# Two metaformer layers on one core: the first transfer, products of ones at the start, and the layout of a convolution's input

## The chip, the core and the metric

The kernel runs on one core of one Trainium2 chip. The core has a matrix engine (PE), a vector engine (DVE), an activation engine (ACT), a general engine (POOL) and a queue that issues transfers (SP). The metric is the device time of one execution in microseconds, as the median of several runs.

## The reference

The input x is 8 images of 384 channels and 32 by 32 points, in float32. There are two layers, each with a token mixer and a feed-forward part:

```
# layer 0
x = x + mamba(ln_c(x))                # input product, causal 3-tap convolution, SiLU,
                                      # selective scan over 1024 tokens (16 states), gate, output product
t = tokens(x);  t = t + ffn0(ln_t(t)) # two products with binarized weights, results clipped by groups of images
# layer 1
x = x + displaced_conv(ln_c(x))       # 48 offsets, each group of 8 channels shifted, then a 5x5 Gaussian
t = tokens(x);  t = t + ffn1(ln_t(t))
```

The feed-forward parts divide the batch into five groups of one image; the images beyond the fifth get zero there. So images 0 to 4 pass through scan, ffn 0, convolution and ffn 1, and images 5 to 7 through scan and convolution alone. The displaced convolution of a channel is separable: one 32 by 32 matrix for the rows and one for the columns, which differ by group of channels.

## The kernel before

All work is first recorded as operations (`op`, `dma`) with an engine, an estimated duration, a key, and the buffers that they read and write. `Flow.run` then plays them against a model of the engines: at each moment an idle engine takes, among the operations whose inputs are ready and whose buffers are free, the one with the lowest key, and the last recorded one where keys are equal. The list `out` that results is issued as it stands, so each engine's order is fixed when the kernel is built. SP's transfers go round eight lanes, and a transfer waits for the one that took its lane before.

Work is tiled in units of one image and 512 tokens (16 units). For each unit: `load_x` brings x (768 KB) into `xn`; `layernorm` (L464 and L484 on PE for sums, L477 and L512 on ACT, L498 and L537 on DVE, L521 and L529 on ACT); `in_proj` (L645) for twelve tiles of output channels; the small convolution and SiLU (ACT L661 to L689, DVE L676); `x_proj` (L760), `prep` (L814, L824, L837); and then, for six tiles and four state groups, `scan` (POOL L868, ACT L878, DVE L893, POOL L914, DVE L927, PE L935). The feed-forward parts of finished images (L1386 and L1465 on PE, L1408 on DVE) and their convolutions are interleaved with the scan of later units; the output product is L997.

At the very start, all transfers of key -60 (x, the small vectors `cw`, `cb`, `bdt`, `dsk`, four pieces of `aneg`, and `wx`, `wdt`) are ready at once; since equal keys take the last recorded, x comes after seven of them. L617 on ACT takes the exponential of `aneg` and needs all four of its pieces.

The displaced convolution (`conv`) works on one image. DVE's L1569 transposes blocks of 32 by 32 from the layer-normed tile `tn` into three tiles `xt`, one for each 128 channels; their free dimension is ordered (row y, channel c). For each of the three, PE's L1601 multiplies with the row matrices: four products of 256 columns, each for 8 of the 32 channels of a block, so the moving operand is read as 8 channels by 32 rows, with y innermost at a step of 32 elements. L1615 (DVE) transposes the result out of PSUM, L1629 (PE) multiplies with the column matrices, L1642 (DVE) transposes back, and L1652 (POOL) adds the residual. Six convolutions lie among the scan, in five stretches, of which the last holds two images (near 865, 1490, 2165, 2785 and 3370 to 3420 us), and two more come at the end, from 3655 us. PSUM has three banks (`mm`) for all products but the scan's.

Of the kernel before, what the change touches and what calls it, by code (L numbers as in the profile page):

```python
# [146 lines left out]
OVER = {"PE": 0.0, "DVE": 0.085, "ACT": 0.1, "POOL": 0.05, "SP": 0.0}  # L147
TIE = 0
RUSH = -40.0
FILL, MARGIN, FIRST = 1e9, 0.8, 45.0  # L150
IDLE, COLD = 2.5, 5.0


class Flow:
# [4 lines left out]
    HOLD = {"exp": 0.0, "silu": 8.77, "gelu": 2.31, "softplus": 0.0}  # L159

    def __init__(self, nc):
        self.nc, self.ops, self.key, self.filler = nc, [], 0.0, None
        self.on = {
            "PE": nc.tensor,
            "DVE": nc.vector,
            "ACT": nc.scalar,
            "POOL": nc.gpsimd,
            "SP": nc.sync,
        }
# [75 lines left out]
    def run(self):  # L245
        nc = self.nc
        waiting = {e: [] for e in self.on}
        busy = {e: 0.0 for e in self.on}
        table, now, out = None, 0.0, []
        events = [0.0]  # L250
        done = []
        dma_free, landed = 0.0, [0.0] * LANES
        idle, cold = 0.0, COLD
        ends = {}
        left = len(self.ops)

        def enter(o):

            new = {}
            for b in o.bufs:  # L260
                if b.slot is None and b.ring.ordered:
                    k = new[b.ring] = new.get(b.ring, 0) + 1
                    if b.n > b.ring.given + k - 1:
                        b.ring.turn.setdefault(b.n - k + 1, []).append(o)
                        return
            insort(waiting[o.eng], (o.key, o.n, o))

        for o in self.ops:
            if o.wait == 0:
                o.ready = 0.0  # L270
                enter(o)
        while left:
            while done and done[0][0] <= now + 1e-9:
                _, _, o = heapq.heappop(done)
                for p in o.next:
                    p.wait -= 1
                    if p.wait == 0:
                        p.ready = now
                        enter(p)
                for b in o.bufs:  # L280
                    b.left -= 1
                    if b.left == 0:
                        b.ring.free.append(b.slot)
                        b.end = now
            moved = False
            nexts = []
            for e, q in waiting.items():
                if busy[e] > now + 1e-9:
                    continue
                best = None  # L290
                for i, (k, n, o) in enumerate(q):
                    if best is not None and (k > best[0] or TIE and k == best[0]):
                        break
                    if o.table is not None and o.table != table:
                        t = o.ready + (self.HOLD[o.table] if o.key > RUSH else 0.0)
                        if now < t - 1e-9:
                            nexts.append(t)
                            continue
                        k += PEN
                        if best is not None and k >= best[0]:  # L300
                            continue
                    if e == "SP" and landed[-LANES] > now + 1e-9:
                        nexts.append(landed[-LANES])
                        break
                    if Ring.open(o.bufs):
                        best = (k, i)
                if best is None:
                    continue
                o = q.pop(best[1])[2]
                for b in o.bufs:  # L310
                    if b.slot is None:
                        b.slot = b.ring.free.pop(0)
                        b.ring.given += 1
                        for p in b.ring.turn.pop(b.ring.given, ()):
                            enter(p)
                us = o.us
                if o.table is not None and o.table != table:
                    us += self.SWITCH
                    table = o.table
                if e == "PE":  # L320
                    if now - idle >= IDLE and (now > FIRST or FILL > 1e6):
                        cold = now + COLD
                    if now < cold - 1e-9:
                        us *= 2
                    if o.us > 0.5:
                        idle = now + us
                busy[e] = now + us
                if e == "SP":
                    dma_free = max(dma_free, now) + (o.lag - 1.8)
                    end = max(dma_free, now + us) + 1.8  # L330
                    landed.append(end)
                else:
                    end = now + us + o.lag
                heapq.heappush(done, (end, o.n, o))
                o.at = now
                if e == "PE":
                    ends[o.n] = now + us
                    for b in o.bufs:
                        b.at = min(b.at, now)
                out.append(o)  # L340
                left -= 1
                moved = True
            if moved:
                continue
            t = [x for x in busy.values() if x > now + 1e-9] + nexts
            if done:
                t.append(done[0][0])
            t = [x for x in t if x > now + 1e-9]
            assert t, "the instructions that are left wait for one another"
            now = min(t)  # L350
        self.end = now
        fills = self.gaps(out, ends) if self.filler else {}
        table = None
        for o in out:
            for b in fills.get(o.n, ()):
                self.filler[2](nc.tensor, b)
            if o.table is not None and o.table != table:
                table = o.table
                nc.scalar.preload_act_table_set(SETS[table])  # L359
            o.fn(self.on[o.eng])  # L360


def metaformer_flow(ctx, tc, x, mw, f0, offset, f1, out):
    nc = tc.nc
    w_in, conv_w, conv_b, w_x, w_dt, b_dt, a_log, d_skip, w_out = mw
    fl = Flow(nc)
# [202 lines left out]

    fl.key = -60  # L570
    load_x(0)
    dma(lambda: cw.ap, lambda: conv_w.rearrange("(j p) t -> p j t", p=P), (), [cw], 10)

    def small(dst, src):
# [971 lines left out]
    def conv(src, dst, dst_ap):  # L1546

        xt = [hb_r.new(2) for _ in range(KC)]
        for s in range(NS):
            last = src is x1[B - 1] and s == NS - 1  # L1550
            if last:
                tn = st[len(units) - 1]["x1"]
            else:
                tn = tn_r.new()
                dma(
                    lambda tn=tn: tn.ap,
                    lambda s=s: halves(src.ap, s),
                    [src[s * KC + k] for k in range(KC)],
                    [tn],
                    768,  # L1560
                )
            layernorm(tn, 1e-6)
            ys = slice(s * T // 32, (s + 1) * T // 32)
            for c in range(KC):

                op(
                    "DVE",
                    0.7,
                    lambda e, c=c, tn=tn, ys=ys: e.transpose(  # L1569
                        xt[c].ap.rearrange("p (y c) -> p y c", c=32)[:, ys, :],  # L1570
                        tn.ap[:, c, :].rearrange("p (y x) -> p y x", x=32),
                    ),
                    [tn],
                    [xt[c][s]],
                )
        for c in range(KC):
# [18 lines left out]
            for h in range(2):  # L1595
                acc = mm.new()

                def ups(e, lt=lts[0], acc=acc, h=h, c=c):
                    for k in (0, 1):
                        cs = slice(h * 16 + k * 8, h * 16 + k * 8 + 8)  # L1600
                        e.matmul(  # L1601
                            acc.ap.rearrange("p (c y) -> p c y", y=32)[:, k * 8 : k * 8 + 8, :],
                            lt.ap[:, 2 * h + k, :],
                            xt[c].ap.rearrange("p (y c) -> p c y", c=32)[:, cs, :],
                            start=True,
                            stop=True,
                        )

                op("PE", 1.0, ups, [lts[0], xt[c]], [acc], hold=[tr])
                hs = slice(h * T, (h + 1) * T)  # L1610

                op(
                    "DVE",
                    0.7,
                    lambda e, tr=tr, acc=acc, hs=hs: e.transpose(  # L1615
                        tr.ap[:, hs].rearrange("p (c x) -> p c x", x=32),
                        acc.ap.rearrange("p (c y) -> p c y", y=32),
                    ),
                    [acc],
                    [tr[h]],  # L1620
                )
# [139 lines left out]
```

## Time and profile before

| | |
|---|---|
| median of 3 runs | 3700.87 us (3692.59 to 3712.57) |
| the profiled execution | 3705.44 us |
| its span, first to last instruction | 3703.7 us |
| mean granted clock of PE | 0.923 |
| L1569, 45 from `tn` and 3 from `xn` | 28.5 and 2.1 us, 677 and 698 ns each |
| L1601, first and last start | 865.5 and 3692.0 us |
| POOL's L868 waiting for PE's L935 | 169.6 us |
| transfers | 777.44 MB, 74.4% of 16 engines' span |

The profile gives for each engine its busy time and share of the span. A group is all instructions of one line, engine and shape: busy us, mean ns of one, idle time ahead of them and what ended it. The chain of work that ended last is followed back from the last instruction, at each step to what released it. A matmul in float32 leaves two records. "To landing" is the time from the issue of a transfer to its data being there. All times are from the start of the span.

### The profile page before, as it was taken

Reading aid. Unit: us, or ns where it says so; the run is one execution under the profiler, and the core shown is the slowest. Engines: PE = TensorE matmul, PEld = TensorE weight load, DVE = VectorE, ACT = ScalarE, POOL = GpSimd, SP = SyncE. Lnnn points to the kernel's source line nnn. Section 1 sums busy time; section 2 is a strip of 40 time slices with the busy share of each in tenths; the row PEclk is TensorE's granted clock in tenths of the full one; section 3 lists DMA queues with packets and bytes.
Section 4 is the critical chain, followed back from the end, with each engine's and each line's share of the span. In section 5 each row is a group of like instructions: output and inputs, shape, how many; then the busy total and the mean of one; then the engine's idle time right before and its main releaser. Section 6 shows DMA issues by size and latency. Waiting matters only on the chain.

```text
span 3703.7 us, 35888 instructions
## 1 busy us (share of the span) xinstructions
PE 3189.1 (86%) x9572; PEld 1143.7 (31%) x9572; DVE 3086.6 (83%) x3080; ACT 2494.7 (67%) x3661; POOL 3157.0 (85%) x1680
## 2 busy tenths in 40 slices
PE   4777878987999897899979789998877999878988
PEld 1222223322333231333323233332223333323334
DVE  2798888878778889997987899889898888788986
ACT  4767886757667676677768757767665676765562
POOL 3879999897697998888899887989998788997893
PEclk7888979998999897999989899999988999988999
DMA  5858778696686886668587776969776787976964
GB/s 145 184 154 223 198 199 221 184 256 181 207 245 175 231 224 181 200 199 243 177 248 205 196 221 193 244 198 255 228 216 195 209 246 225 257 217 207 270 185 155
DMA packets 680820, 777.44 MB, mean 210 GB/s; under 512 B 113689, under 2 KB 434089, under 8 KB 680617
## 3 DMA queue, kind: packets, MB, share of 16 engines
q1 hardware_dynamic: 680616, 775.14, 74.4%
q8 instruction: 77, 1.26, 0.1%
q14 instruction: 127, 1.03, 0.1%
HBM read 578.45 MB, written 196.48 MB: 209 GB/s over the span
## 4 chain that ended last, share of the span: by engine, by line
PE 39%; DVE 16%; DMA 15%; POOL 12%; ACT 10%; issue 6%; SPq 2%; POOLq 0%; DVEq 0%; ACTq 0%
PE mm L1386 10%; PE mm L1465 9%; POOL t L868 8%; PE mm L645 6%; DVE dp L893 5%; PE y L935 4%; DMA dus<-via 3%; PE mm L997 3%; DVE t L893 3%; POOL t L914 3%; DVE t L927 3%; DMA dts<-via 2%; ACT L359 2%; ACT dp L878 2%; PE mm L1601 2%
## 5 line engine op out<-in xcount | busy, mean ns | idle before, releaser
L868 POOL TENSOR_TENSOR t<-dus,bc 128x1024 f32<-128x1024 f32 x768 | 1797.8, 2361 | 209.9 <-PE y L935 169.6
L914 POOL TENSOR_TENSOR t<-t,bc 128x1024 f32<-128x1024 f32 x384 | 906.8, 2362 | 99.6 <-DVE t L893 89.6
L935 PE MATMUL y<-t,sel 128*32 128x512 f32 x3072 | 554.9, 652 | 184.4 <-DVE t L927 117.8
L1465 PE MATMUL mm<-hb,w 128*128 128x512 f32 x1440 | 675.4, 609 | 28.4 <-DMA w<-w2d 12.1
L1386 PE MATMUL mm<-tn,w 128*128 128x512 f32 x1440 | 670.9, 611 | 24.7 <-DMA w<-w1d 7.5
L878 ACT ACTIVATE da<-dts,aneg 128x512 f32<-128x512 f32 x768 | 520.6, 684 | 240.7 <-DVE t L893 216.0
L878 ACT ACTIVATE dp<-dts,aneg 128x512 f32<-128x512 f32 x768 | 528.3, 688 | 207.2 <-DVE t L927 190.3
L893 DVE TENSOR_TENSOR_SCAN dp<-dp,h,t 128x512 f32<-128x512 f32 x384 | 491.3, 1279 | 71.7 <-ACT dp L878 53.5
L893 DVE TENSOR_TENSOR_SCAN dp<-dp,t 128x512 f32<-128x512 f32 x384 | 468.4, 1220 | 90.6 <-ACT dp L878 59.8
L893 DVE TENSOR_TENSOR_SCAN t<-da,h,t 128x512 f32<-128x512 f32 x384 | 481.2, 1267 | 64.2 <-POOL t L868 59.6
L893 DVE TENSOR_TENSOR_SCAN t<-da,t 128x512 f32<-128x512 f32 x384 | 458.2, 1206 | 79.5 <-POOL t L868 68.5
L359 ACT ACT_TABLE_LOAD x391 | 501.7, 1283 | 6.5
L645 PE MATMUL mm<-xn,win 128*128 128x512 f32 x900 | 439.3, 631 | 39.6 <-DMA win<-in_L_conv_in_proj_w 20.5
L927 DVE TENSOR_TENSOR t<-dp,bc 128x1024 f32<-128x1024 f32 x384 | 465.4, 1212 | 8.8 <-ACT h L920 4.0
L1465 PEld LDWEIGHTS mm<-hb,w 128*128 128x128 f32 x1440 | 264.9, 192 | 431.8 <-issue 352.7
L1386 PEld LDWEIGHTS mm<-tn,w 128*128 128x128 f32 x1440 | 269.4, 193 | 413.8 <-issue 311.5
L997 PE MATMUL mm<-z,wo 128*128 128x512 f32 x552 | 276.6, 634 | 12.2 <-DMA wo<-in_L_conv_out_proj_w 7.6
L645 PEld LDWEIGHTS mm<-xn,win 128*128 128x128 f32 x900 | 173.6, 200 | 294.7 <-issue 209.7
L1398 ACT ACTIVATE he<-mm,b 128x512 f32<-128x512 f32 x240 | 162.9, 680 | 148.9 <-PE mm L1386 141.6
L935 PEld LDWEIGHTS y<-t,sel 128*32 128x32 f32 x3072 | 83.4, 112 | 560.0 <-DVE t L927 201.1
L920 ACT COPY h<-dp 128x2 f32<-128x2 f32 x192 | 30.5, 159 | 218.4 <-DVE t L927 112.6
L1408 DVE TENSOR_REDUCE sm<-he 128x1 f32<-128x1024 f32 x120 | 144.3, 1203 | 30.8 <-ACT he L1398 30.2
(133 smaller groups left out, 3170.5 us busy)
## 6 DMA issues: line engine op xcount, KB each, us to landing
dts<-via SPq DMA_DIRECT2D x768, 128.0 KB, 4.4
dus<-via SPq DMA_DIRECT2D x768, 128.0 KB, 4.5
hd<-he SPq DMA_DIRECT2D x120, 512.0 KB, 4.7
hb<-hd SPq DMA_DIRECT2D x120, 512.0 KB, 5.9
via<-soft SPq DMA_DIRECT2D x192, 256.0 KB, 4.3
w<-w2d SPq DMA_DIRECT2D x120, 384.0 KB, 4.7
w<-w1d SPq DMA_DIRECT2D x240, 192.0 KB, 3.9
bc<-bcd SPq DMA_DIRECT2D x256, 128.0 KB, 4.7
```

Of the source, the lines that this page charges most:

```text
L359: nc.scalar.preload_act_table_set(SETS[table])
L645: e.matmul(acc.ap, w.ap[:, k, :], xn.ap[:, k, :], start=(k == 0), stop=(k == KC - 1))
L868: lambda e, t=t, du=du: e.tensor_mul(t.ap, du.ap, wide(0)),
L878: lambda e, c=c, r=r, dt=dt: e.activation(decay(c), dt.ap[:, r, :], AF.Exp, scale=aneg.ap[:, j * Q + c, g : g + 1],),
L893: e.tensor_tensor_scan(t.ap[:, r, :] if p == 0 else decay(c), decay(c), t.ap[:, r, :], 0.0 if s == 0 else hst[j][p].ap[:, g, r : r + 1], A ...
L914: op("POOL", 2.35, lambda e, t=t: e.tensor_mul(t.ap, t.ap, wide(1)), [bc], [t])
L927: lambda e, t=t: e.tensor_mul(t.ap, da[2].ap, wide(1)),
L935: e.matmul(y.ap[c * D : (c + 1) * D, :], sel.ap, ts[c // 2].ap[:, c % 2, :], start=(g == 0), stop=(g == NG - 1), tile_position=(0, c * D),)
L997: e.matmul(o.ap, flat()[:, j, :], zs[j].ap, start=(j == 0), stop=(j == JC - 1))
L1386: e.matmul(acc.ap, w.ap[:, k, :], tn.ap[:, k, :], start=(k == 0), stop=(k == KC - 1),)
L1398: lambda e, he=he, r=r, m=m, acc=acc: e.activation(he.ap[:, r, :], acc.ap, AF.Identity, bias=b1.ap[:, m : m + 1]),
L1465: e.matmul(acc.ap, w.ap[:, part * 2 + r, :], hs[m // 2].ap[:, r * T : (r + 1) * T], start=(m == 0), stop=(m == MC - 1),)
```

## The change

There are three parts.

The transfer of x for the first unit is marked (`lead`) and moved to the head of the issued list. Everything else on SP keeps its order, so the seven small transfers that stood before x now follow it directly.

`FILL` goes from 1e9 to 1.0. With that, `gaps` looks for holes of at least 1 us on PE in the model's first 45 us and puts products of ones (`keep`, 256 columns, into a free bank of `mm`, read by nobody) there. It yields four places: eight products before the first L464, eight between the first L484 and the second L464, seven between the second L484 and the first L645, and three between the third and the fourth product of L645 (26 in all). The first waits for `ones` to be set on POOL. The condition on `cold` in the model says the same as before for both values, so the modelled order stays.

In `conv`, the tile `xt` that L1601 reads is ordered (k, y, c) with four k and eight c in place of (y, c). L1569 writes it so, in runs of 8 elements; L1601's moving operand is then 256 contiguous elements; its result in PSUM is ordered (k, y, c), and L1615 reads it with y innermost at a step of 8 elements. What L1615 writes, and L1629, L1642 and L1652, are as before.

The order of the instructions on ACT and POOL is unchanged; on DVE only the shape of L1569 and L1615 differs, and on PE only the 26 products are new.

```diff
-FILL, MARGIN, FIRST = 1e9, 0.8, 45.0
+FILL, MARGIN, FIRST = 1.0, 0.8, 45.0
...
-        self.nc, self.ops, self.key, self.filler = nc, [], 0.0, None
+        self.nc, self.ops, self.key, self.filler, self.lead = nc, [], 0.0, None, None
...
-                    if now - idle >= IDLE and (now > FIRST or FILL > 1e6):
+                    if now - idle >= IDLE:
                         cold = now + COLD
...
         fills = self.gaps(out, ends) if self.filler else {}
         table = None
+        out.sort(key=lambda o: o is not self.lead)
         for o in out:
             for b in fills.get(o.n, ()):
                 self.filler[2](nc.tensor, b)
...
     fl.key = -60
     load_x(0)
+    fl.lead = fl.ops[-1]
...
                     lambda e, c=c, tn=tn, ys=ys: e.transpose(
-                        xt[c].ap.rearrange("p (y c) -> p y c", c=32)[:, ys, :],
-                        tn.ap[:, c, :].rearrange("p (y x) -> p y x", x=32),
+                        xt[c].ap.rearrange("p (k y c) -> p y k c", k=4, c=8)[:, ys],
+                        tn.ap[:, c, :].rearrange("p (y a b) -> p y a b", a=4, b=8),
                     ),
...
                     for k in (0, 1):
-                        cs = slice(h * 16 + k * 8, h * 16 + k * 8 + 8)
                         e.matmul(
-                            acc.ap.rearrange("p (c y) -> p c y", y=32)[:, k * 8 : k * 8 + 8, :],
+                            acc.ap[:, k * 256 : k * 256 + 256],
                             lt.ap[:, 2 * h + k, :],
-                            xt[c].ap.rearrange("p (y c) -> p c y", c=32)[:, cs, :],
+                            xt[c].ap[:, (2 * h + k) * 256 : (2 * h + k + 1) * 256],
...
-                        tr.ap[:, hs].rearrange("p (c x) -> p c x", x=32),
-                        acc.ap.rearrange("p (c y) -> p c y", y=32),
+                        tr.ap[:, hs].rearrange("p (k c x) -> p k c x", k=2, x=32),
+                        acc.ap.rearrange("p (k y c) -> p k c y", k=2, c=8),
```

## The prediction

> **What bounds the kernel now.** I read the busy shares first, then the chain of work that ended last, then the groups with their shapes kept apart, then the first 50 us of the timeline, and last the windows around the five places where the convolution runs.
>
> ```profile
> PE 3189.1 (86%) x9572; PEld 1143.7 (31%) x9572; DVE 3086.6 (83%) x3080; ACT 2494.7 (67%) x3661; POOL 3157.0 (85%) x1680
> PE 39%; DVE 16%; DMA 15%; POOL 12%; ACT 10%; issue 6%; SPq 2%; POOLq 0%; DVEq 0%; ACTq 0%
> PE mm L1386 10%; PE mm L1465 9%; POOL t L868 8%; PE mm L645 6%; DVE dp L893 5%; PE y L935 4%; DMA dus<-via 3%; PE mm L997 3%; DVE t L893 3%; POOL t L914 3%; DVE t L927 3%; DMA dts<-via 2%; ACT L359 2%; ACT dp L878 2%; PE mm L1601 2%
> ```
>
> No engine is the bound: PE, POOL and DVE lie within 3% of one another, and the chain changes between them. L1601, the product that the change rewrites, holds 2% of the chain (74 us by the rounded share), though all its records together are only 89.2 us busy: nearly all of it ended last somewhere.
>
> ```profile
> L1386 PE MATMUL mm<-tn,w 128*128 128x512 f32 x1440 | 670.9, 611 | 24.7 <-DMA w<-w1d 7.5 <-DVE tn L537 6.4 <-ACT he L1398 4.4
> L1601 PE MATMUL mm<-hb,lt 128*128 128x256 f32 x192 | 89.2, 615 | 13.0 <-DVE hb L1569 8.4 <-DVE hb L1642 4.1 <-DVE xn L498 0.5
> L1629 PE MATMUL mm<-hb,lt 128*128 128x128 f32 x384 | 52.9, 289 | 7.3 <-DVE hb L1615 3.2 <-ACT dp L878 1.3 <-DVE hb L1642 0.9
> L1615 DVE STREAM_TRANSPOSE hb<-mm 128x512 f32<-128x512 f32 x48 | 33.8, 706 | 24.2 <-PE mm L1601 21.7 <-ACT mm L529 2.4
> L1642 DVE STREAM_TRANSPOSE hb<-mm 128x512 f32<-128x512 f32 x48 | 32.8, 692 | 6.3 <-PE mm L1629 6.1 <-ACT da L878 0.2
> ```
>
> The column after the bar is busy us and the mean ns of one record (an fp32 product leaves two). L1601 streams 256 columns and takes 615 ns, as L1386 does for 512; L1629, which reads runs of 16, takes 289 for 128. In the timeline L1601's weight loads stand 0.43 us apart, as with 512 columns elsewhere, and L1629's 0.11. So L1601's read, one element every 128 bytes, runs at half rate.
>
> ```profile
> 5.20 0.55 SPq L217 DMA_DIRECT2D xn<-in_x  x1
> 10.87 1.93 PE L464 MATMUL mm<-xn,ones 128*32 128x512 f32 x6 [10.87 <-DMA xn<-in_x]
> 14.78 0.54 SPq L576 DMA_DIRECT2D aneg<-in_L_conv_A_log  x1
> 20.17 0.28 ACT L617 ACTIVATE aneg<-aneg 128x96 f32<-128x96 f32 x1
> 26.88 4.75 PE L645 MATMUL mm<-xn,win 128*128 128x512 f32 x6 [3.21 <-DVE xn L537]
> 31.47 2.74 PE L645 MATMUL mm<-xn,w 128*128 128x512 f32 x6
> ```
>
> At the start everything waits for x, which is the eighth transfer. The first input product takes 4.75 us at 26.88 and the next one 2.74: 4.2 us of work pass before PE's records go from 0.855 to 0.43 us apart.
>
> ```profile
> core 0: us, PE busy (x) PEld busy (x) DVE busy (x) ACT busy (x) POOL busy (x), PEclk, DMA share, GB/s
> 880.00:900.00 20.00, 19.61 (x69) 8.80 (x68) 19.17 (x24) 12.64 (x26) 13.35 (x7) 1.00 0.53 173
> 1490.00:1510.00 20.00, 19.68 (x66) 9.49 (x67) 20.00 (x25) 8.60 (x14) 19.79 (x12) 0.91 0.65 208
> 3672.00:3698.00 26.00, 20.34 (x81) 13.65 (x80) 13.40 (x21) 1.38 (x2) 9.35 (x4) 0.87 0.67 221
> ```
>
> Where a convolution lies among the scan, DVE or POOL is as full as PE; in the tail only PE is.
>
> **The product, priced.** A record goes from 0.435 us to twice L1629's spacing for twice its columns, 0.22: 0.215 saved, times 192 is 41 us of PE, 5.2 for each of eight convolutions. The group's mean should fall from 615 to about 400 ns. How much moves the end is read stage by stage.
>
> Tail (two convolutions, from 3655). I followed the timeline: L1601's eight records at 3657.61, 3665.95, 3683.34 and 3688.93 and four at 3677.25 hold DVE's L1615 or PE's own queue. The first saves 1.7; the second's gain is lost, since DVE's L1569 waits for POOL's L1652 there, which only shifts; the four at 3677.25 save 0.9, the last two groups 1.7 each. The weights (lt) of the last group are issued when the group before ends, and take 1.9 us, so they move with it. Sum 6 us.
>
> Among the scan (six convolutions). PE's gain cannot shorten a stretch below its fullest other engine. I took twelve windows of 20 us over the five stretches, and in each 20 less the larger of DVE and POOL: 1.3, 0.8, 0.2 (from 860); 0.0, 0.6 (1490); 2.1, 0.0 (2160); 2.9, 0.6 (2780); 3.5, 1.3, 1.2 (3365). That is 14.5 of PE's 31; the rest PE spends waiting for DVE or POOL. Not every idle piece of DVE waits for L1601, so I take 9, with 0 and 28 as ends (28: the chain's L1601 pieces there, some 56 us, halved).
>
> **The transposes.** L1569 now writes runs of 8, L1615 reads PSUM at 32-byte steps; 48 of each, order kept. L1642 already reads PSUM at 64-byte steps, at 692 ns against 706 for L1615's contiguous read: no price, so I take 0. [...] L1569's write has no such row; its bounds are 0 and a doubling (32 us of DVE).
>
> **x first, and the fill.** Issued at 0.74 with 5.0 to 5.5 us to landing (rows of xn), x is there by 6. But PE now begins with eight products of ones, 16 records of 256 columns, as soon as ones is set (3.2): 0.43 each cold, 0.22 warm. With the trace's 4.2 us to warm: ten cold to 7.4, six warm to 8.7. [...] I keep 8.7: the fill, not x, sets PE's start, 2.2 us earlier than 10.87. L464 and L484, warm, take 1.06 and 1.0 instead of 1.93 and 2.08, so DVE's L498 starts at 11.6 instead of 15.59. The second fill of eight, 3.5 us, fits the hole there (15.55 to 18.91).
>
> Then a wait appears that was covered. ACT has L617 ahead of the second L477, and L617 needs the fourth aneg transfer: issued at 14.78, 5.0 us to landing, so 19.8, just ahead of 20.17. Its place in SP's queue is kept, and it waits there for landings; the small transfers now stand behind x. I put it at 19.3 (18.5 to 20.5). ACT would be there at 16.2; it waits 3 us, and L477 behind it starts at 19.6, not 20.95. PE is idle from 16.1 to 20.3 and cold again (at 51.65 a pair of L760 takes 1.97 us after 2.16 us idle, 1.07 otherwise). L484 runs cold to 22.4; the third fill, 14 records, five cold, nine warm, ends at 26.4, where xn is ready at 25.6: it costs 0.8. The first L645, warm, ends at 29.0, not 31.47: 2.5 us gained. The fourth fill (three products, 1.3 us) stands before the fourth L645, where the trace has no hole (36.62); what follows waits for u from ACT (39.98), so I count 0, at worst 1.3. Start: 2.5, from 0 to 6; it shifts all that follows, as all of it descends from x.
>
> **Sum.** 2.5 + 9 + 6 = 17.5 us. On the profiled execution: 3705.4 - 17.5 = 3687.9; that execution was 4.6 above the median of the three runs, so 3683.4 on the median. I say 3683; from the stage's bounds this case reaches from 3672 to 3692.
>
> **Rivals.**
> Most of the chain passes: DVE's and POOL's work in those windows can move earlier along with PE, whose lead is kept beyond them. For it speaks that POOL waits 169.6 us for PE's L935; against it, windows like 1490 to 1510 with DVE at 20.00. 28 + 6 + 2.5 = 36: 3665. Chance 0.20.
> Only start and tail count, or the read was not what held L1601: 8.5 us at most, 3693. For it, the full windows. Chance 0.22.
> DVE takes over: the four-dimensional patterns of L1569 and L1615 run at half speed. 96 x 0.69 = 66 us more of DVE, where it is 82 to 100% busy; the tail's idle DVE covers some, leaving 50 to 55, less 8: 3746. From 0.18 us a transpose (17.5 / 96) the gain is gone, from 0.37 it is slower by over 0.5%. Against it, L1642's row. Chance 0.08.
> The forecast keeps 0.50.
>
> A measurement of this kernel tells about 0.5% (18.5 us) from no change, so the line lies at 3682.4, across the middle of the forecast's own range. Faster: 0.20 and half of 0.50, with a little of the rest, 0.47; slower 0.08; same 0.45. The range takes in the first rival and the second, and leaves out the third: 3664 to 3699.
>
> **What would show it.** L1601's mean near 400 ns (615 if the read was not the cause). L1615 and L1569 still near 0.68 to 0.71. L617 waiting for aneg at about 19.3, the first L645 at 26.4 and 2.7 us long, x in SBUF before PE's first fill is over. Around 1500 and 2170 PE newly idle, waiting for DVE or POOL. Wrong if L617 starts at 16, or if those windows shrink by PE's whole 5 us.

## The result and the profile after

The kernel after takes 3689.21 us (median of 14 runs, 3683.65 to 3699.24), the kernel before, run beside it, 3702.14 us (14 runs, 3691.71 to 3712.57). The ratio is 0.9964, with a 95% interval of 0.9954 to 0.9974: 13.3 us less [9.6 to 17.0]. That is real, and inside the half per cent that the prediction called no change. Run again beside the later experiments, the same kernel took 3694.07 us, against 3707.28 us for the one before (0.9966 [0.9950, 0.9981]). The profiled execution took 3689.18 us, with a span of 3687.4 us and a mean granted clock of 0.919.

The first part of the page after, and its chain of waits:

```profile
PE 3174.9 (86%) x9624; PEld 1156.4 (31%) x9624; DVE 3087.3 (84%) x3080; ACT 2495.3 (68%) x3661; POOL 3157.5 (86%) x1680
PE 32%; DVE 15%; DMA 11%; POOL 11%; ACT 7%; issue 5%; SPq 1%; POOLq 0%; DVEq 0%; ACTq 0%
PE mm L1388 9%; PE mm L1467 9%; POOL t L870 7%; DVE dp L895 5%; PE y L937 4%; PE mm L647 4%; DVE t L895 3%; DMA dus<-via 3%; DVE t L929 2%; PE mm L999 2%; DMA dts<-via 2%; POOL t L916 2%; ACT dp L880 2%; ACT L360 2%; DMA bc<-bcd 1%
```

The busy times of DVE, ACT and POOL are those of before, to within 1 us. The row convolution, L1601 before and L1602 now, is no longer among the lines that the page lists of the chain. The shares of this chain add up to 82% only, so its other entries are not to be set against those of before.

The groups with their shapes kept apart:

```profile
L1602 PE MATMUL mm<-hb,lt 128*128 128x256 f32 x192 | 54.2, 422 | 16.2 <-DVE hb L1571 9.6 <-DVE hb L1643 4.8 <-DVE xn L538 0.8
L1630 PE MATMUL mm<-hb,lt 128*128 128x128 f32 x384 | 53.0, 286 | 14.2 <-DVE hb L1616 7.9 <-DVE hb L1643 1.4 <-ACT dp L880 1.3
L1616 DVE STREAM_TRANSPOSE hb<-mm 128x512 f32<-128x512 f32 x48 | 33.0, 695 | 5.2 <-PE mm L1602 4.4
L1571 DVE STREAM_TRANSPOSE hb<-tn 128x512 f32<-128x512 f32 x45 | 28.6, 677 | 0.6 <-POOL hb L1653 0.6
L407 PE MATMUL mm<-ones 128*128 128x256 f32 x52 | 16.8, 493 | 3.2 <-POOL sm L1150 3.2
```

The row convolution fell from 89.2 to 54.2 us of PE, 615 to 422 ns a record. Both transposes cost what they did (695 after 706, 677 after 677). The waits have changed sides. The transpose out of PSUM had waited 21.7 us for PE, now 4.4; the column product L1630 waits 7.9 us for that transpose, where its group (L1629 before) waited 3.2. PE used to be late here, and now DVE is. L407, the products of ones, is new: 16.8 us of PE at the start.

The same three of the windows as before, each moved to where its work now lies:

```profile
core 0: us, PE busy (x) PEld busy (x) DVE busy (x) ACT busy (x) POOL busy (x), PEclk, DMA share, GB/s
876.00:896.00 20.00, 19.81 (x80) 10.03 (x79) 19.50 (x24) 13.02 (x28) 12.65 (x6) 1.00 0.53 173
1485.00:1505.00 20.00, 20.00 (x70) 10.42 (x69) 20.00 (x25) 8.42 (x15) 18.16 (x12) 0.86 0.66 219
3656.00:3682.00 26.00, 16.48 (x87) 13.29 (x86) 14.09 (x22) 1.38 (x2) 9.56 (x4) 0.87 0.72 240
```

In the first two PE is at least as busy as it was (19.61 and 19.68 before): where its product got shorter, later work moved up (80 records where 69 were, 70 where 66 were). DVE, which was all but full there, stays so: 19.50 of 20 after 19.17, and 20.00 in the second before and after. In that second window PE's granted clock is also lower, 0.86 after 0.91; whether part of PE's fullness there is the clock, no run shows. In the tail PE's busy time fell from 20.34 to 16.48 us of 26 and nobody's rose much: PE's gain became PE's idle time.

The first 33 us of the timeline (start, length, and in brackets the idle time ahead and what ended it):

```profile
0.73 0.44 SPq L217 DMA_DIRECT2D xn<-in_x  x1
3.19 6.62 PE L407 MATMUL mm<-ones 128*128 128x256 f32 x16 [3.19 <-POOL sm L1150]
9.74 1.06 PE L465 MATMUL mm<-xn,ones 128*32 128x512 f32 x6
...
19.52 0.28 ACT L619 ACTIVATE aneg<-aneg 128x96 f32<-128x96 f32 x1 [2.29 <-DMA aneg<-in_L_conv_A_log]
20.33 2.08 PE L485 MATMUL mm<-sq,pick 96*128 96x512 f32 x2 [3.27 <-ACT sq L478]
22.20 5.15 PE L407 MATMUL mm<-ones 128*128 128x256 f32 x14
27.19 2.74 PE L647 MATMUL mm<-xn,win 128*128 128x512 f32 x6
29.76 2.74 PE L647 MATMUL mm<-xn,w 128*128 128x512 f32 x6
```

The new wait for `aneg` stands where it was predicted, and L485 behind it runs cold: 2.08 us, with a granted clock of 0.50 from 20.0 to 26.0 us, where `aneg_soon` (below) has 1.12 us. The second input product starts at 29.76 us and not at 31.47: 1.7 us gained here.

### The profile page after: what moved, and what is told of

The parts are those of the page before. It is cut to its first block, busy times and chain, and to the rows that moved or that the text cites. A ratio compares the mean times of both kernels' runs of the same rounds, so it can differ in the third digit from the quotient of the medians.

```text
span 3687.4 us, 35993 instructions
## 1 busy us (share of the span) xinstructions
PE 3174.9 (86%) x9624; PEld 1156.4 (31%) x9624; DVE 3087.3 (84%) x3080; ACT 2495.3 (68%) x3661; POOL 3157.5 (86%) x1680
## 4 chain that ended last, share of the span: by engine, by line
PE 32%; DVE 15%; DMA 11%; POOL 11%; ACT 7%; issue 5%; SPq 1%; POOLq 0%; DVEq 0%; ACTq 0%
PE mm L1388 9%; PE mm L1467 9%; POOL t L870 7%; DVE dp L895 5%; PE y L937 4%; PE mm L647 4%; DVE t L895 3%; DMA dus<-via 3%; DVE t L929 2%; PE mm L999 2%; DMA dts<-via 2%; POOL t L916 2%; ACT dp L880 2%; ACT L360 2%; DMA bc<-bcd 1%
## 5 line engine op out<-in xcount | busy, mean ns | idle before, releaser
L1467 PE MATMUL mm<-hb,w 128*128 128x512 f32 x1440 | 687.3, 618 | 30.2 <-DMA w<-w2d 15.0
```

Source lines behind the costliest of these rows:

```text
L1467: e.matmul(acc.ap, w.ap[:, part * 2 + r, :], hs[m // 2].ap[:, r * T : (r + 1) * T], start=(m == 0), stop=(m == MC - 1),)
```

## The experiments

A figure in us is the ratio's distance from 1, times the median of the kernel before that ran beside it. "Kernel after" means the changed kernel; line numbers shift by one or two from kernel to kernel.

| kernel | median, us | ratio to before | us from before |
|---|---|---|---|
| `layout_only` | 3696.13 | 0.9975 [0.9964, 0.9986] | -9.3 [-13.3, -5.2] |
| `start_only` | 3701.93 | 0.9989 [0.9975, 1.0003] | -4.1 [-9.3, +1.1] |
| `pe_time_back` | 3701.79 | 0.9988 [0.9977, 0.9999] | -4.4 [-8.5, -0.4] |
| `half_product` | 3687.38 | 0.9949 [0.9931, 0.9967] | -18.9 [-25.6, -12.2] |
| `aneg_soon` | 3685.07 | 0.9934 [0.9915, 0.9953] | -24.4 [-31.5, -17.4] |
| `tail_swap` | 3691.77 | 0.9965 [0.9950, 0.9979] | -13.0 [-18.5, -7.8] |
| `lead_only` | 3701.70 | 0.9993 [0.9979, 1.0007] | -2.6 [-7.8, +2.6] |
| `fill_only` | 3695.06 | 0.9969 [0.9955, 0.9984] | -11.5 [-16.7, -5.9] |
| `after_again` | 3694.07 | 0.9966 [0.9950, 0.9981] | -12.6 [-18.5, -7.0] |
| `start_trimmed` | 3689.41 | 0.9951 [0.9933, 0.9969] | -18.2 [-24.8, -11.5] |
| `dve_twice` | 3717.53 | 1.0032 [1.0018, 1.0045] | +11.9 [+6.7, +16.7] |

### The layout without the new start

```diff
-FILL, MARGIN, FIRST = 1.0, 0.8, 45.0
+FILL, MARGIN, FIRST = 1e9, 0.8, 45.0
...
-        out.sort(key=lambda o: o is not self.lead)
```

> The new layout of the convolution's input alone; x is the eighth transfer again and PE has no products of ones. My theory (the product's shorter time is worth what DVE, POOL and the last transfers leave free): the change's gain less the 1.7 us that its start shows, about 11 us under the kernel before, 3691; the first L645 at 26.9 and 4.75 us long as before; L1602 (the product) at 422 ns. Rival A (the gain is the start's, carried on): within 2 us of before. Rival B (all of the chain's share passes): 3668.

It takes 9.3 us off. Its profiled execution (3707.15 us) is the second slowest of its 17 runs, 11 us above their median, so only its local rows are used. They show the turn of the waits as in the kernel after: 8.0 us of waiting for the transpose at the column product, and 433 ns a record at the row convolution.

```profile
L1601 PE MATMUL mm<-hb,lt 128*128 128x256 f32 x192 | 55.9, 433 | 16.2 <-DVE hb L1570 8.3 <-DVE hb L1642 5.9 <-DVE xn L537 0.8
L1629 PE MATMUL mm<-hb,lt 128*128 128x128 f32 x384 | 53.8, 290 | 14.2 <-DVE hb L1615 8.0 <-DMA lt<-ltd 2.1 <-ACT dp L879 1.3
```

### The new start without the layout

The same kernel as after, with the four old patterns of `conv`:

```diff
-                            acc.ap[:, k * 256 : k * 256 + 256],
+                            acc.ap.rearrange("p (c y) -> p c y", y=32)[:, k * 8 : k * 8 + 8, :],
...
-                            xt[c].ap[:, (2 * h + k) * 256 : (2 * h + k + 1) * 256],
+                            xt[c].ap.rearrange("p (y c) -> p c y", c=32)[:, cs, :],
```

> x first and the products of ones, with the old layout of the convolution's input. My theory: 1.7 us under before (ratio 0.9995), not to be told from it; second L645 at 29.8 us as in the changed kernel. Rival A: the whole 13 us, 3689.

It takes 4.1 us off, with an interval that takes in zero. With the 9.3 of the layout that makes 13.4, against 13.3 for the whole change. The two parts add, as far as these intervals can tell. The timeline of the start again:

```profile
20.26 1.13 PE L485 MATMUL mm<-sq,pick 96*128 96x512 f32 x2 [3.71 <-ACT sq L478]
21.23 4.87 PE L407 MATMUL mm<-ones 128*128 128x256 f32 x14
25.94 2.74 PE L647 MATMUL mm<-xn,win 128*128 128x512 f32 x6
28.51 2.74 PE L647 MATMUL mm<-xn,w 128*128 128x512 f32 x6
```

The instructions on PE up to here are those of the kernel after, yet L485 is warm (1.13) after 3.71 us of idling, where the profile of after had it cold after 3.27. So the cold product is a matter of the single execution, not of the kernel, and so is 1.25 us of the gain at the start. Nor is the pause free where L485 is warm: the fill behind it takes 4.87 us here for the 14 records that take 3.19 in `aneg_soon`. PE went cold a little later, while it was busy: its granted clock is 1.00 up to 21.5 us and 0.50 from 22.0 to 25.0.

### PE's time given back

Ahead of each product of the row convolution stands a product of ones into the same bank. The new layout and the transposes stay. The second product of ones of each pair lands on the first product's result, so half of the row convolution's result is sums of ones.

```diff
                     for k in (0, 1):
+                        keep(e, acc.ap)
```

> The changed kernel, with two unread products of ones (256 columns) in each pair of row products, into the bank that the pair then overwrites: 0.86 us of PE each, just what the contiguous read saves, and nothing else put back. My theory (PE's time in the convolution is the cause): as start_only, within 3 us. Rival C (the gain comes from the transposes or from where DVE's and POOL's work falls): stays at the changed kernel's 3689.

```profile
L1617 DVE STREAM_TRANSPOSE hb<-mm 128x512 f32<-128x512 f32 x48 | 33.9, 707 | 26.3 <-PE mm L1603 26.2
```

The transpose out of PSUM waits 26.2 us for PE again (21.7 before the change, 4.4 after it), PE's whole busy time goes to 3190.6 us, that of `start_only` being 3192.3, and the time comes back with it: 0.9988, against 0.9989 for `start_only`. The two ratios are equal to within some 6.5 us by their intervals; against the kernel after, 8.9 us are lost, plus or minus 5.5. So what the layout gains is PE's time, and not something that it does to DVE or to the memory.

### Half of the row convolution left out

Only the first product of each pair is issued; the other half of each result stays what the bank held.

```diff
-                    for k in (0, 1):
+                    for k in (0,):
```

> The changed kernel with one of the two row products of each pair left out (half of the row convolution isn't computed, its half of the bank holds what was there): PE saves another 96 records of 0.22, 21 us. My theory (after the change DVE, POOL and transfers hold the convolutions): at most 4 us under the changed kernel, 3685 to 3689. Rival B (PE's products still end last there): in proportion to the first 41 us, 13 x 21 / 41 = 7 us, 3682, or more.

The group falls from 54.2 to 33.1 us of PE, and the ratio by 0.0015 more than in the kernel after: 5.6 us, plus or minus 8. This was to tell whether the gain was used up, and it does not: a rate of 5.6 in 21 is as good as that of the change itself, and zero is in the interval too. The waits lean the way of "used up" (20.5 us ahead of the group, where the kernel after has 16.2), but waits are no price.

### The transfer that the start waits for

The last of the four `aneg` transfers is issued right behind x.

```diff
-        out.sort(key=lambda o: o is not self.lead)
+        out.sort(key=lambda o: 0 if o is self.lead else 1 if o in self.soon else 2)
...
+        fl.soon.append(last_aneg)
```

> The changed kernel with the four transfers of aneg right behind x, ahead of the other small ones. My theory (behind x and the products of ones, ACT's wait for aneg is what the start now stands on): ACT's L620 at 17.3 us, not 19.5; L486 right after, warm, at 18; xn ready at 22.4, the third row of products of ones over by then; the first L648 at 22.5, not 27.2, and the whole 4 to 5 us under the changed kernel (ratio to before 0.995). Rival (PE's cold clock or the other small transfers hold the start): first L648 later than 25.

The timeline of its start:

```profile
17.11 0.28 ACT L620 ACTIVATE aneg<-aneg 128x96 f32<-128x96 f32 x1
17.91 1.12 PE L485 MATMUL mm<-sq,pick 96*128 96x512 f32 x2 [0.99 <-ACT sq L478]
18.87 3.19 PE L407 MATMUL mm<-ones 128*128 128x256 f32 x14
22.25 2.84 PE L648 MATMUL mm<-xn,win 128*128 128x512 f32 x6 [0.19 <-DVE xn L538]
```

The wait is gone, L485 is warm, and the first input product starts at 22.25 us instead of 27.19, as expected. The median, of six runs, gains more than those 5 us: 24.4, where the kernel after gained 13.3 beside its own kernel before. That is 11 more, but the interval, 17 to 32 us, does not exclude 13.3 and 5.

### The wait in the tail taken away

In the tail the profile of after has a new long wait on DVE:

```profile
3665.36 0.38 SPq L217 DMA_DIRECT2D tr<-x  x1
...
3670.82 0.69 DVE L1537 TENSOR_TENSOR tr<-tr,mm 128x512 f32<-128x512 f32 x1 [3.00 <-DMA tr<-x]
...
3671.42 0.71 DVE L1616 STREAM_TRANSPOSE hb<-mm 128x512 f32<-128x512 f32 x1
...
3672.19 2.08 PE L1630 MATMUL mm<-hb,lt 128*128 128x128 f32 x8 [4.05 <-DVE hb L1616]
```

The last residual add of the feed-forward waits 3.00 us for its x, where it waited 0.40 before (the line below); the transpose L1616, whose input is ready, stands behind it on DVE, and PE idles 4.05 us for that. My theory was that this wait takes most of what the tail gains. The edit puts the next instruction of DVE, that transpose, ahead of the add. The line of the kernel before, and the edit:

```profile
3686.38 0.69 DVE L1535 TENSOR_TENSOR tr<-tr,mm 128x512 f32<-128x512 f32 x1 [0.40 <-DMA tr<-x]
```

```diff
+        i = out.index(self.late)
+        j = next(n for n in range(i + 1, len(out)) if out[n].eng == "DVE")
+        out.insert(i, out.pop(j))
```

> The changed kernel with one pair of DVE's instructions exchanged near the end: the transpose of the product's result (L1620) goes ahead of the residual's addition (L1541) that waits 3.0 us for its transfer tr. My theory (this wait ate the tail's gain): from DVE's last L503 to the end of the span 45 us instead of 47.6 (50.2 before the change). Rival (the transfers lt and hb hold the tail as well): within 1 us of 47.6.

The line named there as L503 should be the normalizing step on DVE (L537 before, L538 after), from whose last instructions on `tn` (3653.53 us before, 3639.83 after) the tail is counted. The tail is 47.5 us, against 47.6 in the kernel after, and the ratio is the same (0.9965). The theory falls. The same place in the timeline shows why:

```profile
3661.29 1.58 DVE L1620 STREAM_TRANSPOSE hb<-mm 128x512 f32<-128x512 f32 x2 [0.39 <-PE mm L1606]
...
3663.84 0.69 DVE L1541 TENSOR_TENSOR tr<-tr,mm 128x512 f32<-128x512 f32 x1 [0.97 <-DMA tr<-x]
...
3664.78 1.13 PE L1634 MATMUL mm<-hb,lt 128*128 128x128 f32 x8 [2.66 <-DMA lt<-ltd]
...
3666.47 1.97 PE L1606 MATMUL mm<-hb,lt 128*128 128x256 f32 x8 [0.56 <-DMA lt<-ltd]
```

Both transposes now run before the add, and PE is no longer held by them. It waits for its weights `lt` instead (2.66 and 0.56 us), which come by the same queue.

### x first without the fill

The kernel after with the old patterns of `conv` and `FILL` at 1e9.

> x as the first transfer and nothing else of the change. My theory: PE's first product at 6 to 6.5 us instead of 10.87, DVE's L499 at 11, but ACT's exponential of aneg waits to about 19.5 as in the changed kernel; the first L646 cold at about 25.7, the second at 30.3 instead of 31.5: 1.2 us gained. Rival (no such wait): first L646 at 22.

```profile
5.72 1.93 PE L465 MATMUL mm<-xn,ones 128*32 128x512 f32 x6 [5.72 <-DMA xn<-in_x]
...
19.73 0.28 ACT L619 ACTIVATE aneg<-aneg 128x96 f32<-128x96 f32 x1 [4.71 <-DMA aneg<-in_L_conv_A_log]
...
25.82 4.64 PE L647 MATMUL mm<-xn,win 128*128 128x512 f32 x6 [3.21 <-DVE xn L538]
30.30 2.74 PE L647 MATMUL mm<-xn,w 128*128 128x512 f32 x6
```

The early part came as expected. x is there at 5.72 us, 4 us before the fill lets PE go in the kernel after, and it brings nothing, since ACT then waits 4.71 us for `aneg` instead of 2.29. What is left, 1.2 us at the second input product (30.30 against 31.47), can't be told from nothing at the end (0.9993 [0.9979, 1.0007]).

### The fill without x first

The kernel after with the old patterns and without the sort.

> The products of ones alone, x as the eighth transfer, old layout. My theory: the first products are over at 9.8 and x comes at 10.9; DVE's L498 at 14, ACT's exponential waits for aneg to 19.8, and the second L645 starts at 30 instead of 31.5: 1.5 us gained, as with x first; the two parts of the start are not additive. Rival (x first is the part that counts): no gain.

```profile
20.38 1.12 PE L484 MATMUL mm<-sq,pick 96*128 96x512 f32 x2 [2.46 <-ACT sq L477]
...
28.63 2.74 PE L646 MATMUL mm<-xn,w 128*128 128x512 f32 x6
```

The second input product starts at 28.63 us, 2.8 us earlier than before and not 1.5: in this execution the product that is L485 elsewhere (L484 here) was warm (1.12 us) after 2.46 us of idling. `start_only`, with the same product warm and x first added, has 28.51. So beside the fill, x first brings 0.1 us at this place: the wait for `aneg` takes the rest.

The median, 11.5 us under before in only 7 runs, is more than `start_only` gives with x first added to it (4.1). The intervals overlap from 5.9 to 9.3. Part of the distance goes along with the clock: over all their runs `fill_only` has a mean granted clock of 0.9240 and `start_only` 0.9213, and among the runs of one kernel 0.001 less of it goes with some 1.6 us more (245 runs of all kernels, correlation -0.58). By that slope, an estimate, 4 of the 7 us are the clock's. Why the clock differs stays open.

### The changed kernel again, and its start mended

> The changed kernel once more, as the base of the two others on the same chip: 0.9964 of the kernel before, within its interval of 0.001. L1616 must be near 695 ns and L1602 near 422.

It repeats within the interval. The tail is 48.0 us, the transpose L1616 695 and now 700 ns. The next kernel is `aneg_soon` with two products of ones fewer in the first hole and none in the short one:

```diff
-                        fills[o.n] = [ring.slots[s]] * n
+                        fills[o.n] = [ring.slots[s]] * (n - 2 if last == 0.0 else n if n > 5 else 0)
```

> The changed kernel with the aneg transfers right behind x, two products of ones fewer at the start (six) and none before the fourth input product. First PE product of x at about 8.0 us instead of 9.7 (9.6 with the aneg transfers alone moved); ACT's L620 at 15.6 if aneg is there, the first L648 at 20.7. 6 to 7 us of start under the changed kernel; the whole 5 to 10 us under it, if the start is passed on. Rival (a shift of the start is lost in the scan): equal to the changed kernel.

L465 starts at 8.38 us and the first input product at 21.02 (8.0 and 20.7 were expected), another 1.2 us under `aneg_soon`. At the end it is 5.6 us under the changed kernel, plus or minus 8.8, so that neither the expected 5 to 10 us nor its rival, no gain, is excluded. Both mended starts beat the changed kernel in their ratios. For `aneg_soon` the intervals just part (0.9953 at its upper end, 0.9954 at the lower end of the changed kernel's first result), and the two mended starts can't be told apart from one another.

### The other engine, for its price

The transpose out of PSUM is done twice; nothing else is changed.

```diff
-                    lambda e, tr=tr, acc=acc, hs=hs: e.transpose(
+                    lambda e, tr=tr, acc=acc, hs=hs: [
+                        e.transpose(
...
+                        for _ in range(2)
+                    ],
```

> The changed kernel with each of the 48 transposes L1616 done twice: 33 us more of DVE, 25 of them among the scan. My theory (DVE's own work is what the convolutions stand on once PE is faster): most of it passes, 15 to 25 us over the changed kernel. Rival (no engine alone holds them; each us of any engine is worth about a quarter, as PE's 41 us were worth some 10): 8 us over it.

```profile
L1617 DVE STREAM_TRANSPOSE hb<-mm 128x512 f32<-128x512 f32 x96 | 67.0, 705 | 6.0 <-PE mm L1602 4.3
...
L1633 PE MATMUL mm<-hb,lt 128*128 128x128 f32 x384 | 59.4, 311 | 27.9 <-DVE hb L1617 21.0 <-DVE hb L1646 2.9 <-ACT da L880 2.0
```

DVE's group grows from 33.3 (in `after_again`) to 67.0 us, and the time by 0.0066 of 3707, 24.5 us, plus or minus 8: 0.73 us for each us of DVE, from 0.49 to 0.96. The rival of the expectation, 8 us, lies outside. PE's row convolution gave back 9.3 us for 35.0, 0.27 for each, from 0.15 to 0.38. That is a price for time removed, but `pe_time_back` has one for time added at the same place: 192 records of 0.215 us, 41 us of PE, lost 8.9 us, 0.22 for each, from 0.08 to 0.35. So by either measure an us of PE is worth much less here than an us of DVE. The second transpose also stands between the two products, so 0.73 is the price of DVE's time at this place and not of DVE's time anywhere.

## Why the prediction was right, point by point

The direction and the mechanism were right, and the size was somewhat too large: 3683 was said, with 3672 to 3692 for the forecast's own case, and 3689 measured. The sum was 17.5 us, and 13.3 [9.6, 17.0] came, so the sum lies just outside the interval. (How the lower end of the range, 3672, comes from the stages' bounds is not worked out; the ends that the prediction gives for the scan would put it at 3664.) Faster by over half a per cent was given a chance of 0.47, no change by that measure 0.45, and no change is what came.

**The product.** The predicted mean was about 400 ns, the measured one 422; 35.0 us of PE went instead of 41. `pe_time_back` shows that this time is the cause of the layout's gain.

**Among the scan** (9 predicted). The layout gives 9.3 [5.2, 13.3] with its part of the tail, which is 1.5 us by the mean of profiles (below); that leaves about 7.8. The stages say the same. This is the time in us from the start of a convolution's first transpose out of PSUM (L1615) to that of its last transpose back (L1642), for the eight convolutions in turn:

| kernel | 1 | 2 | 3 | 4 | 5 | 6 | sum of six | 7 | 8 |
|---|---|---|---|---|---|---|---|---|---|
| before | 36.1 | 35.3 | 19.9 | 26.4 | 23.3 | 24.0 | 165.0 | 42.6 | 18.4 |
| `pe_time_back` | 36.8 | 35.4 | 19.8 | 26.4 | 23.3 | 24.0 | 165.7 | 41.8 | 20.1 |
| after | 34.4 | 34.8 | 17.0 | 24.1 | 21.8 | 23.3 | 155.4 | 39.9 | 18.0 |
| `layout_only` | 34.2 | 34.9 | 17.4 | 24.2 | 22.1 | 23.3 | 156.1 | 40.5 | 18.4 |

The six among the scan are 9.6 and 8.9 us shorter with the new layout, and as long as before when PE's time is given back. (The other executions with the old layout have 0.4 to 1.4 us more than before, the other complete ones with the new layout 6.4 to 10.3 less.) No stretch shrank by PE's whole 5 us, which would have been the sign of being wrong. The windows had 2.3, 0.6, 2.1 and 3.5 us of room in the first four stretches, and 1.7, 0.5, 2.9 and 2.3 came; in the last, with two convolutions, they had 6.0, and 2.2 came. So of PE's time about a third passes there, 9.6 of 26 us, until DVE is full. That the sum came out at 9 is in part luck: the windows gave 14.5, and the cut from there to 9 was a judgement without working.

The sign that I named for it, PE newly idle around 1500 and 2170 us, showed in one place of two. Around 1500 PE is 20.00 of 20 busy, since work from behind moved up. Around 2170, the window of before and the one of after that begins as far ahead of its convolution:

```profile
2160.00:2180.00 20.00, 20.00 (x76) 10.78 (x75) 17.89 (x21) 9.72 (x15) 9.87 (x5) 1.00 0.77 213
2157.00:2177.00 20.00, 19.42 (x93) 11.90 (x91) 19.05 (x23) 10.68 (x15) 12.28 (x6) 1.00 0.88 251
```

PE has 0.6 us of idle time there that it did not have, and DVE is fuller. In the waits the turn is plain: 7.9 us for L1616 at the column product.

**The tail** (6 predicted) is the term that was too large. From the last layer norm to the end:

| kernels | tail, us |
|---|---|
| old layout: before, `start_only`, `lead_only`, `fill_only` | 50.2, 51.1, 49.9, 50.1 |
| new layout: after, `after_again`, `layout_only`, `aneg_soon`, `start_trimmed` | 47.6, 48.0, 48.6, 49.8, 50.2 |

The means are 50.3 and 48.8: 1.5 us, and the best single one of these 2.6. `pe_time_back`, with 50.9, is back among the old ones. These are single executions, and the new ones scatter by 2.6 us. The table of stretches shows where the term failed: the seventh convolution is 2.1 to 2.7 us shorter, and the eighth, whose last two groups were to save 1.7 each, is not (18.0 and 18.4, where it was 18.4). The groups of the row convolution were taken to end last one after another, each with its 1.7 us. With PE faster, the transfers that PE and DVE need there are late next (DVE waits 3.00 us for `tr` in the kernel after, PE 2.66 us for `lt` in `tail_swap`); I had taken that into account for the last `lt` only. `tail_swap` shows that one such wait taken away makes room for the next. That the queue as a whole is the limit there is only argued; no run gave the tail its data earlier.

**The transposes** at nothing: right, 695 and 677 ns. No run here shows a price for DVE's read at 32-byte steps: 695 ns in the kernel after and 700 in `after_again`, against 706 for the contiguous read before.

**The start** (2.5 predicted): 1.7 in the profile of after, and between 1.0 and 3.0 in the other executions with the same start (second input product at 30.48 in `after_again`, 30.13 in `pe_time_back`, 28.79 in `half_product`, 28.51 in `start_only`). Three of its steps were right: the fill and not x lets PE go; L619 waits for `aneg`, until 19.52 (said: 19.3); L485 behind it is cold until 22.4. The last is in part luck, since `start_only` had it warm. Two were a little short. The first fill ended at 9.74 us, not 8.7, and the third cost 1.6 us instead of 0.8, as PE took longer to warm than the 4.2 us read from the trace of before. From 3.19 to the start of L465 at 9.74, 16 records took 6.55 us; at 0.435 and 0.22 that is, as an estimate, 14 cold ones, some 6.1 us. The same fill in other executions let L465 start at 9.23 (`start_only`), 8.59 (`after_again`) and 8.34 us (`pe_time_back`), by the same working 5.1, 3.8 and 3.3 us of cold. So 8.7 lay within what executions differ by, 8.34 to 9.74.

By the end the start seems to be worth more than at 30 us: 4.1 us by `start_only`, 4.0 by difference (13.3 less 9.3), though the interval of the first, -9.3 to +1.1, takes in the 1.7 as well. One place where it grows can be seen: SP's issue of twelve transfers `bc` in the kernel before, after, and with the new start alone:

```profile
80.71 13.16 SPq L217 DMA_DIRECT2D bc<-bcd  x12
```

```profile
78.98 11.42 SPq L217 DMA_DIRECT2D bc<-bcd  x12
```

```profile
78.07 10.51 SPq L217 DMA_DIRECT2D bc<-bcd  x12
```

They start 1.7 and 2.6 us earlier than before, and are out 3.5 and 5.3 us earlier; in `layout_only`, whose start is the old one, they take 13.08 us. POOL's L868 waits 8.90 us for `bc` before, 7.92 after, and 7.07 in `start_only`. Why a shift of 2 us shortens the row of twelve isn't settled. Nor can the traces show how much of this lead survives. It wanders by 5 us either way from stage to stage: at 3467 us the kernel after is 10.8 ahead of before, the same kernel again 14.4, and `layout_only`, in its execution of 3707 us, 4.8 behind. For parts of this size only medians count.

**The clock** was not in the sum. Over all runs the kernel after has a mean granted clock of 0.9204 and 0.9207 (twice measured) and `layout_only` 0.9207, where the kernel before has 0.9220 to 0.9229. By the slope given at `fill_only`, an estimate, that is 2 to 4 us, so part of what PE's shorter product gained may be lost there. It is a correlation; no run tests it.

**The rivals.** Most of the chain passing (3665) falls: 9.3 of 35 passed. DVE taking over falls with the transposes' rows. Only start and tail counting (3693) falls by its mechanism: the layout gives 9.3 us, its tail 1.5 to 2.6 of that, and the six stretches among the scan are 6 to 10 us shorter. In time it was the closest of all, 4 us off where the forecast's own 3683 was 6 off. That nearness is no support for it, since its tail was taken at 6 us and its scan at nothing.

## What to carry to other kernels

Time saved on one engine came through here only about as far as its neighbours in the same stage had room (among the scan, 9.6 us where the windows had 14.5): count the neighbours' idle time in windows of that stage, not the saved engine's share of the chain (about 0.27 us came back for each us of PE taken away, and about 0.73 was lost for each us of DVE added). When a transfer is moved to the front, look at once for the next transfer that an engine's next instruction waits for (here ACT's, 2.29 us for `aneg`): x first and the fill together brought the start 1.7 us, x first beside the fill hardly anything (28.51 against 28.63 us), and moving one small `aneg` up behind x another 5. Where the last stage is fed by one queue, don't add up the waits of a faster engine there one by one: when `tail_swap` took one wait away, the next transfer was late, by 2.66 us, and the sum of 6 us stood against 1.5 by the mean of profiles.

## What the runs showed of the hardware

DVE's transpose of 128x512 float32 out of PSUM took no longer with a read at 32-byte steps (695 ns in the kernel after, 700 in `after_again`, 707 in `pe_time_back`, where it waits 26.2 us for PE, 21.7 before) than with a contiguous one (706 before).

PE's float32 product with a moving operand of one element every 128 bytes took 615 ns a record of 256 columns (before), and 422 with contiguous elements (after).

Whether PE was cold after a pause did not follow from the pause alone here. The same product, L485, was warm after 2.46 us (1.12 us, `fill_only`) and 3.71 us (1.13, `start_only`), between the two after 4.20 us (1.37, `half_product`), and cold after 3.27 us (2.08, after) and 4.85 us (2.08, `pe_time_back`). In `fill_only` and `start_only` the fill behind the warm product then took 4.87 us for 14 records, against 3.19 in `aneg_soon`; in the first two the granted clock was 0.50 from 22.0 to 25.0 us.

The twelve issues on SP near 80 us took from 9.99 us (`aneg_soon`) to 13.16 us (before), with the same transfers, as their start moved from 73.39 to 80.71 us.
